# Layer 3's experts moved into the slots of layer 3's attention, with gelu built from tanh

## The chip, the cores and the metric

The kernel runs on one core of a Trainium2 chip. A core has a tensor engine for matrix products (PE, with its weight loads shown as PEld), a vector engine (DVE), a scalar engine for activation functions (ACT), a third elementwise engine (GpSimd, shown as POOL), and a queue that issues DMA transfers (SyncE, SP). The engines run side by side and wait for each other through semaphores. The metric is the device time of the whole program in microseconds (us); lower is better.

## What is computed

The input `x` has 2048 tokens of 256 numbers, and the context has 1601 rows of 256. Four layers follow each other. Each adds a cross attention and then a feed-forward part to `x`, both on a layer norm of `x`. The change concerns the last layer. Its attention has 16 heads of 16 numbers, and its mask leaves the last 400 context rows. Its feed-forward part has 8 experts; expert `e` handles the tokens 256e to 256e+255, so no routing is computed.

```python
def _L3_xattn_ref(query, key, value, mask, Wq, bq, Wk, bk, Wv, bv, Wo, bo):
    ...
    scores = jnp.einsum('bhqd,bhkd->bhqk', Q, K) / jnp.sqrt(jnp.float32(DK))
    scores = jnp.where(mask == 0, -jnp.inf, scores)
    weights = jax.nn.softmax(scores, axis=-1)
    attn = jnp.einsum('bhqk,bhkd->bhqd', weights, V)
    attn = attn.transpose(0, 2, 1, 3).reshape(b, -1, D)
    return attn @ Wo.T + bo

def _L3_ffn_ref(x, w1, b1, w2, b2):
    ...
    tokens = x.reshape(E, T, D)
    h = jnp.einsum('etd,edf->etf', tokens, w1) + b1[:, None, :]
    h = jax.nn.gelu(h)
    y = jnp.einsum('etf,efd->etd', h, w2) + b2[:, None, :]
    return y.reshape(B, S, D)
...
x = x + _L3_xattn_ref(_layernorm(x, axis=-1), ctx_1024, ctx_1024, mask, ...)
x = x + _L3_ffn_ref(_layernorm(x, axis=-1), L3_ffn_w1, L3_ffn_b1, L3_ffn_w2, L3_ffn_b2)
```

`jax.nn.gelu` is here the form with tanh, 0.5h(1 + tanh(0.79788(h + 0.044715h^3))).

## The kernel before

`x` stays on the chip as 16 tiles of 128 tokens. Four tiles make a chunk of 512 tokens, so there are four chunks, and each chunk holds the tokens of two experts. `norm` (L125) makes a chunk's layer norm: statistics on DVE (L132, L133), the inverse root on POOL (L135, L136), the normalised rows on DVE (L142), then eight transposes on PE (L161) through the `pm` bank, which ACT copies to `xnT` (L165).

`attention3_tail` (L1415) is layer 3's attention. A unit is one chunk and one group of four heads, so there are 16 units. A unit has four slots, one for each block of 100 context rows, hence 64 slots `n`, with `u, kt = divmod(n, 4)`. In each slot PE computes `scores` (L1564, four heads side by side into two score tiles `psc`), ACT takes `exp` of each of the two (L1571), and PE multiplies the exps of the previous slot by the values (`values`, L1581). Besides, each slot computes two pairs of row maxima for the token tile six ahead: `maxima` (matmul L1546 into a `psc` tile, DVE reduction L1550). Once per unit come `project` for the unit two ahead (L1531, copied twice by ACT, L1535 and L1536), `shift` (L1557, L1558), and `normalize` of the unit just ended (L1595): ACT copies its sums to `ri` (L1597), four `reciprocal` calls on DVE follow (L1604), and POOL multiplies (L1606). After a chunk's last unit come four `out_project` calls (L1614), which add to `x` (L1618 on POOL, L1619 on DVE). Finished unit ends wait in the lists `tasks`, `pieces` and `later`.

PE's order is the order in which the program states its instructions (`manual_schedule`, L1518); the order on the other engines is made by a scheduler from dependencies and the program's order. `banks` (L1517) divides PSUM: three score tiles of two banks each, one bank `pm` shared by project, shift, normalize, out_project and the norm's transposes, and one for the sums of values. The next chunk's norm is stated at once, at the slots 4, 20 and 36.

`ffn3` (L1649) runs after it. For each expert it loads `w1`, `w2` (1 MB each) and `b2` into one of three buffers, and for every second expert makes a chunk's norm. Per expert it does 8 column blocks of `w1` (L1702), gelu of each by one ACT instruction with the bias `b1` (L1706), then for the two token tiles the product with `w2` (L1713), adds `x + b2` (POOL L1718, DVE L1719) and stores `y` (L1720).

The core of the slot loop before is

```python
scores(u, kt)
maxima(n + 6, 0)
if last is not None:
    values(*last)
last = (u, kt)
maxima(n + 6, 1)
```

Of the kernel before, what the change touches and what calls it, by code (L numbers as in the profile page):

```python
# [8 lines left out]
F32 = mybir.dt.float32  # L9
# [3 lines left out]
ALU = mybir.AluOpType  # L13
# [40 lines left out]
class Net:  # L54
# [70 lines left out]
    def norm(self, c, row_scale=None, rms=False, split=None):  # L125


        nc = self.nc
        st = self.small.tile([P, TPC, 6], F32, name="st")
        mv = self.small.tile([P, TPC, 2], F32, name="mv")  # L130
        for i in range(TPC):
            nc.vector.bn_stats(st[:, i, :], self.x[c * TPC + i])  # L132
            nc.vector.bn_aggr(mv[:, i, :], st[:, i, :])  # L133
        rstd = self.small.tile([P, TPC], F32, name="rstd")
# [5 lines left out]
        for i in range(TPC):  # L140
# [4 lines left out]
            xns.append(xn)  # L145
        if rms:
# [5 lines left out]
            for i in range(TPC):  # L152
                nc.vector.tensor_scalar(xns[i], xns[i], ri[:, i : i + 1], None, ALU.mult)
        if split is None:
# [14 lines left out]
        return xnT  # L169
# [1245 lines left out]
    def attention3_tail(self, mask):  # L1415
# [6 lines left out]
        with ExitStack() as s:  # L1422
            kv = s.enter_context(tc.tile_pool(name="kv3", bufs=1))
            qp = s.enter_context(tc.tile_pool(name="q3", bufs=3))
            pp = s.enter_context(tc.tile_pool(name="p3", bufs=6))
# [45 lines left out]
            with ExitStack() as s0:  # L1471
# [7 lines left out]
                wvT = kv.tile([P, 2, D], F32, name="wvT")  # L1479
# [37 lines left out]
            self.banks(s, s=3, m=1, a=1)  # L1517
# [92 lines left out]
            def out_project(c, i):  # L1610
# [8 lines left out]
                nc.vector.tensor_tensor(x, ps[:, :D], x, ALU.add)  # L1619

            def normed(c):
                xnT[c] = self.norm(c)


            tasks, later, pieces = [], [], []
            normed(0)
# [8 lines left out]
            for n in range(U * TK):  # L1635
                u, kt = divmod(n, TK)
                scores(u, kt)
                maxima(n + 6, 0)
                if last is not None:
                    values(*last)  # L1640
                last = (u, kt)
                maxima(n + 6, 1)
                if kt == 0 and u + 2 < U:
                    project(u + 2)
# [5 lines left out]
                elif later:  # L1650
                    f, args = later.pop(0)
                    f(*args)
                    if kt == 3 and later:
                        f, args = later.pop(0)
                        f(*args)
                if pieces:
                    reciprocal(*pieces.pop(0))
                if n % (G * TK) == TK and u // G + 1 < NCH:
                    normed(u // G + 1)
            values(*last)  # L1660
            for f, args in tasks:
                f(*args)
            for args in pieces:
                reciprocal(*args)
            for f, args in later:
                f(*args)

# [56 lines left out]
def network(ctx: ExitStack, tc: tile.TileContext, a, out):  # L1724
# [7 lines left out]
    with tc.If(n_odd == 0) as masked:  # L1732
# [4 lines left out]
        net.attention3_tail(masks[1])  # L1737
        net.ffn3()
# [42 lines left out]
```

## Time and profile before

| | us |
|---|---|
| median of three runs | 2224.9 (2219.83 to 2228.75) |
| the profiled execution | 2223.65 |
| its span, first to last instruction | 2221.9 |
| layer 3's first scores | at 1778.3 |
| layer 3's last values end | at 2088.9 |

The mean granted clock of PE over the span is 0.936 of full speed. A group line of the profile names the source line, the engine, the operation and the tiles, then the busy time and the mean duration of one, then the idle time ahead of it and what ended it. The groups of layer 3 that matter most, over the part of the trace from 1500 us on:

```profile
L1571 ACT ACTIVATE p<-psc 100x1024 f32<-100x1024 f32 x128 | 125.5, 1023 | 110.1 <-PE psc L1564 104.5 <-PE psc L1546 5.5
L1550 DVE TENSOR_REDUCE ms<-psc 128x2 bf16<-128x800 f32 x128 | 124.1, 987 | 67.2 <-PE psc L1546 63.0 <-PE psc L1564 3.5
L1702 PE MATMUL psc<-xnT,w 128*128 128x256 f32 x256 | 57.5, 381 | 1.4 <-ACT h L1706 1.0 <-ACT xnT L165 0.2
L1713 PE MATMUL pa<-w,h 128*128 128x256 f32 x256 | 56.6, 379 | 0.0
```

One f32 matmul appears as two records. Records overlap on PE, so their mean duration is longer than their share of the time.

### The profile page before, as it was taken

How to read it: one execution, taken by the hardware profiler on the slowest of the kernel's cores; microseconds unless marked ns; L12 is line 12 of the kernel's file. 1: busy time of each engine (PE TensorE's matmuls, PEld its weight loads, DVE VectorE, ACT ScalarE, POOL GpSimd, SP SyncE). 2: the span in 40 equal slices, each digit the busy share in tenths (PEclk: the TensorE clock that was granted, in tenths of full speed). 3: DMA queues.
4: the chain of work that ended last, by engine and by line, in shares of the span. 5: the costliest groups of instructions: out<-in, count | busy, mean ns of one | idle time of the engine just before them, and what ended most of it. 6: DMA issues, size and time to landing. Idle time of an engine off the chain costs nothing.

```text
span 2221.9 us, 22832 instructions
## 1 busy us (share of the span) xinstructions
PE 1968.0 (89%) x8841; PEld 967.7 (44%) x8841; DVE 1209.1 (54%) x2252; ACT 717.5 (32%) x968; POOL 632.3 (28%) x405
## 2 busy tenths in 40 slices
PE   7789999999998677789897889999968788989899
PEld 3233333333334422234443674555557422333487
DVE  4565646555552599975645563222076557566500
ACT  4544434344443100000112442111143255455422
POOL 1168878777785000000000021000024401000100
PEclk9799999999998699999997899999978889799999
DMA  8820000000000000000201000000000000000351
GB/s 278 265 83 1 1 1 1 1 1 1 1 1 0 1 0 1 1 0 0 67 0 40 0 1 21 0 1 1 0 0 1 6 1 1 1 1 1 114 188 61
DMA packets 39698, 63.51 MB, mean 29 GB/s; under 512 B 5133, under 2 KB 32158, under 8 KB 39582
## 3 DMA queue, kind: packets, MB, share of 16 engines
q1 hardware_dynamic: 37776, 60.33, 8.4%
q10 hardware_dynamic: 1806, 1.64, 0.2%
q8 instruction: 71, 1.16, 0.2%
q14 instruction: 45, 0.37, 0.1%
HBM read 59.87 MB, written 2.10 MB: 28 GB/s over the span
## 4 chain that ended last, share of the span: by engine, by line
PE 66%; DVE 22%; ACT 4%; issue 3%; DMA 3%; POOL 2%; SPq 0%; DVEq 0%; ACTq 0%; POOLq 0%
PE pa L454 7%; PE psc L442 5%; PE psc L627 5%; PE psc L766 4%; PE pa L786 4%; DVE ge L576 4%; DVE mp L367 4%; PE psc L1564 3%; PE psc L1702 3%; DVE ge L578 2%; PE pa L1713 2%; DVE ri L404 2%; PE pa L1581 2%; DVE ri L1604 2%; PE pm L1614 2%
## 5 line engine op out<-in xcount | busy, mean ns | idle before, releaser
L463 POOL TENSOR_TENSOR sp<-sp,p 128x1024 f32<-128x1024 f32 (+1 forms) x176 | 418.9, 2380 | 59.6 <-ACT p L447 49.0
L367 DVE TENSOR_REDUCE mp<-pm 128x1 f32<-128x512 f32 x384 | 242.6, 679 | 161.4 <-PE pm L362 160.7
L447 ACT ACTIVATE p<-psc 128x1024 f32<-128x1024 f32 (+1 forms) x208 | 212.9, 1024 | 261.1 <-PE psc L442 167.0
L442 PE MATMUL psc<-qT,kT 64*128 64x512 f32 (+1 forms) x832 | 219.9, 591 | 0.0
L454 PE MATMUL pa<-p,v 128*64 128x512 f32 (+1 forms) x832 | 204.2, 613 | 0.0
L593 PE MATMUL psc<-ge,pick 128*8 128x512 bf16 x512 | 142.3, 378 | 37.9 <-DVE ge L576 18.6
L1571 ACT ACTIVATE p<-psc 100x1024 f32<-100x1024 f32 x128 | 125.5, 1023 | 110.1 <-PE psc L1564 104.5
L1550 DVE TENSOR_REDUCE ms<-psc 128x2 bf16<-128x800 f32 x128 | 124.1, 987 | 67.2 <-PE psc L1546 63.0
L362 PE MATMUL pm<-kb,qb 64*128 64x512 bf16 x384 | 100.2, 389 | 26.4 <-DVE mp L367 24.9
L1564 PE MATMUL psc<-q,kT 32*100 32x512 f32 x512 | 97.8, 689 | 14.8 <-DVE ms L1550 10.3
L627 PE MATMUL psc<-w_e,xe 128*128 128x512 f32 x256 | 110.4, 593 | 0.0
L454 PEld LDWEIGHTS pa<-p,v 128*64 128x64 f32 (+1 forms) x832 | 51.1, 137 | 131.6 <-issue 128.6
L135 POOL TENSOR_SCALAR rstd<-mv 128x4 f32<-128x4 f32 x32 | 10.5, 329 | 333.6 <-DVE mv L133 333.6
L829 POOL MEMSET v<- 128x4 f32 x1 | 0.1, 106 | 366.4 <-DVE n_odd L280 366.4
L766 PE MATMUL psc<-q,kT 128*128 128x512 f32 (+1 forms) x208 | 102.2, 610 | 0.0
L576 DVE TENSOR_SCALAR ge<-bc,g 128x128 bf16<-128x128 f32 (+15 forms) x128 | 99.8, 780 | 1.8 <-ACT bc L570 1.8
L142 DVE TENSOR_SCALAR xn<-x,mv,rstd 128x256 f32<-128x256 f32 x128 | 54.3, 482 | 75.0 <-PE pm L161 72.1
L442 PEld LDWEIGHTS psc<-qT,kT 64*128 64x128 f32 (+1 forms) x832 | 85.5, 185 | 19.5 <-issue 6.3
L786 PE MATMUL pa<-v,p 128*128 128x257 f32 (+1 forms) x416 | 93.9, 381 | 0.0
L593 PEld LDWEIGHTS <-pick 128*8 128x8 bf16 x512 | 39.4, 85 | 117.3 <-issue 91.3
L578 DVE TENSOR_SCALAR ge<-bc,g 128x1920 bf16<-128x1920 f32 (+14 forms) x120 | 89.4, 746 | 0.6 <-ACT bc L570 0.6
L440 PE MATMUL psc<-sh,negz 64*128 64x512 bf16 (+1 forms) x416 | 87.1, 383 | 2.6 <-ACT sh L389 2.5
(343 smaller groups left out, 3250.5 us busy)
## 6 DMA issues: line engine op xcount, KB each, us to landing
w<-in_L_ffn_w_dram SPq DMA_DIRECT2D x16, 1024.0 KB, 6.2
head<-in_mask_BxSxS_ik_dram SPq DMA_DIRECT2D x16, 600.5 KB, 4.7
head<-in_mask_1x1xSxS_ik_dram SPq DMA_DIRECT2D x16, 600.5 KB, 4.8
tail<-in_mask_BxSxS_ik_dram SPq DMA_DIRECT2D x16, 200.0 KB, 4.5
tail<-in_mask_1x1xSxS_ik_dram SPq DMA_DIRECT2D x16, 200.0 KB, 3.7
x<-in_x_dram SPq DMA_DIRECT2D x16, 128.0 KB, 3.7
w_e<-in_L_ffn_experts_dram SPq DMA_DIRECT2D x2, 1024.0 KB, 7.2
out_dram<-y SPq DMA_DIRECT2D x16, 128.0 KB, 2.7
```

Of the source, the lines that this page charges most:

```text
L367: nc.vector.tensor_reduce(mp[:, i, j, n : n + 1], pair[j][:, :wd], AX.X, ALU.max)
L442: nc.tensor.matmul(sc[:r, j, :], lhsT=kT[h, hp, kt * P : kt * P + r], rhs=q[h, :], start=False, stop=True,)
L447: nc.scalar.activation(p[:r], sc[:r], AF.Exp, scale=DH**-0.5)
L454: nc.tensor.matmul(acc[h, :], lhsT=v[:r, kt, hp * P + h.start : hp * P + h.stop], rhs=p[:r, j, :], start=kt == 0, stop=kt == NKT - 1,)
L463: nc.gpsimd.tensor_tensor(sums[:r], sums[:r], p[:r], ALU.add)
L576: nc.vector.tensor_scalar(ge[:, :hi], bc[:, :hi], own, None, ALU.is_lt)
L578: nc.vector.tensor_scalar(ge[:, hi:], bc[:, hi:], own, None, ALU.is_le)
L593: nc.tensor.matmul(rk[j // 2][0:E, j % 2, :], lhsT=pick[:, e, :], rhs=ge[:, j * CH : (j + 1) * CH], start=first, stop=last,)
L627: nc.tensor.matmul(sc[:, j, :], lhsT=xnT[t // TPC][:, kc, (t % TPC) * P : (t % TPC + 1) * P], rhs=ew[kc][:, half * 4 + 2 * j : half * 4 + ...
L766: nc.tensor.matmul(sc[:r, j, :], lhsT=kT[:, kc, ks], rhs=q[:, kc, :], start=kc == 0, stop=False)
L786: nc.tensor.matmul(acc[:, : D + 1], lhsT=p[:r, kt, i * P : (i + 1) * P], rhs=v[:r, kt, :], start=kt == 0, stop=kt == NKT - 1,)
L1564: nc.tensor.matmul(sc[j // 2][:TR, j % 2, :], lhsT=kT[h, g, kt * TR : (kt + 1) * TR], rhs=q[u][h, :], start=True, stop=True,)
```

## The change

`attention3_tail` becomes `layer3_tail`, and in this branch of the program `ffn3` is no longer called: the experts run inside the attention loop. When the last `out_project` of chunk `c` is stated, `feed_forward(c)` puts 38 steps into the list `fbits`: one `begin`, five `norm_step`, and for each of two experts eight `up` and eight `down`. Each slot takes two steps from it, by `feed(1)` between the two maxima and `feed(1)` at its end. What is left runs after the loop.

`up` writes one block's product into half of a PSUM tile of one bank; ACT adds the bias, and after each second block POOL makes z = h(0.044715h^2 + 1) in three instructions. `gelu` takes tanh on ACT and makes (tanh + 1)h on DVE. The missing factor 0.5 is applied in `end`, where DVE scales the sum. `down` adds one block's product for both token tiles in a second bank. To make room, the score tiles go from three to two, the p3 buffers from six to five, `wvT` borrows an `attn3` tile, and expert weights have two buffers instead of three; the first two experts are loaded ahead of the loop.

In a slot, `values` moves ahead of the first maxima, `reciprocal` to the top, and `out_project` is no longer confined to slots without another task. The layer norm becomes a generator of six steps, `norm_steps`; `norm` drains it. In the loop the next chunk's norm takes one step per slot from the slots 0, 16 and 32 on.

```diff
+    def norm_steps(self, c, out, row_scale=None, rms=False, split=None):
...
         for i in range(TPC):
             nc.vector.bn_stats(st[:, i, :], self.x[c * TPC + i])
             nc.vector.bn_aggr(mv[:, i, :], st[:, i, :])
+            if i % 2:
+                yield
...
             xns.append(xn)
+            if i == 1:
+                yield
...
+        yield
         if split is None:
             xnT = self.xnp.tile([P, 2, CH], F32, name="xnT")
...
+            if kc == 0:
+                yield
+        out.append(xnT)
...
-            pp = s.enter_context(tc.tile_pool(name="p3", bufs=6))
+            pp = s.enter_context(tc.tile_pool(name="p3", bufs=5))
...
-            self.banks(s, s=3, m=1, a=1)
+            self.banks(s, s=2, m=1, a=1)
+            psf = s.enter_context(tc.tile_pool(name="ps_f", bufs=1, space=bass.MemoryType.PSUM))
+            wp = s.enter_context(tc.tile_pool(name="f3w", bufs=2))
+            hp = s.enter_context(tc.tile_pool(name="f3h", bufs=2))
...
+            for e in range(2):
+                load_expert(e)
...
+                if i == TPC - 1:
+                    fbits.extend(feed_forward(c))
...
+                def up(e, f, k):
+                    w1 = experts[e][0]
+                    if k == 0:
+                        if f == 0:
+                            state["h"] = hp.tile([P, NF, 256], F32, name="h3")
+                        state["ps"] = psf.tile([P, 2, 256], F32, name="psu", tag="u")
+                    ps = state["ps"][:, k, :]
+                    for kc in range(2):
+                        nc.tensor.matmul(
+                            ps, lhsT=w1[:, kc, (f + k) * P : (f + k + 1) * P],
+                            rhs=out[0][:, kc, (e % 2) * 256 : (e % 2 + 1) * 256],
+                            start=kc == 0, stop=kc == 1,
+                        )
+                    at = e * NF + f + k
+                    h = state["h"][:, f : f + 2, :]
+                    nc.scalar.activation(h[:, k, :], ps, AF.Identity, bias=b1[:, at : at + 1])
+                    if k == 1:
+                        z = hp.tile([P, 2, 256], F32, name="z3")
+                        nc.gpsimd.tensor_tensor(z, h, h, ALU.mult)
+                        nc.gpsimd.tensor_scalar(z, z, 0.044715, 1.0, ALU.mult, ALU.add)
+                        nc.gpsimd.tensor_tensor(z, z, h, ALU.mult)
+                        gelus.append((h, z))
...
+                def down(e, f, k):
...
+                    for i in range(2):
+                        nc.tensor.matmul(
+                            acc[:, i, :], lhsT=state["h"][:, f + k, i * P : (i + 1) * P], rhs=w2[:, f + k, :],
+                            start=f + k == 0 and i == 0, stop=f + k == NF - 1 and i == 1,
+                        )
...
+                def end(e):
...
+                        nc.gpsimd.tensor_tensor(y, self.x[t], b2, ALU.add)
+                        nc.vector.scalar_tensor_tensor(y, state["acc"][:, i, :], 0.5, y, ALU.mult, ALU.add)
+                        nc.sync.dma_start(self.out[0, t * P : (t + 1) * P, :], y)
+                    if e + 2 < E:
+                        load_expert(e + 2)
...
+                for e in (2 * c, 2 * c + 1):
+                    for f in range(0, NF + 4, 2):
+                        for k in range(2):
+                            if f < NF:
+                                yield up, (e, f, k)
+                        for k in range(2):
+                            if f >= 4:
+                                yield down, (e, f - 4, k)
+
+            def gelu():
+
+                if gelus:
+                    h, z = gelus.pop(0)
+                    nc.scalar.activation(z, z, AF.Tanh, scale=0.7978845608028654)
+                    nc.vector.scalar_tensor_tensor(h, z, 1.0, h, ALU.add, ALU.mult)
...
             for n in range(U * TK):
                 u, kt = divmod(n, TK)
+                if pieces:
+                    reciprocal(*pieces.pop(0))
                 scores(u, kt)
-                maxima(n + 6, 0)
                 if last is not None:
                     values(*last)
                 last = (u, kt)
+                maxima(n + 6, 0)
+                feed(1)
                 maxima(n + 6, 1)
+                gelu()
...
-                elif later:
+                if later:
                     f, args = later.pop(0)
                     f(*args)
...
-                if pieces:
-                    reciprocal(*pieces.pop(0))
-                if n % (G * TK) == TK and u // G + 1 < NCH:
-                    normed(u // G + 1)
+                feed(1)
+                if n % (G * TK) == 0 and u // G + 1 < NCH:
+                    norming = self.norm_steps(u // G + 1, xn)
+                step(norming, 1)
...
+            while pieces:
+                reciprocal(*pieces.pop(0))
+                feed(2)
+                gelu()
...
+            while fbits:
+                ready = len(gelus)
+                feed(2)
+                for _ in range(ready):
+                    gelu()
...
-        net.attention3_tail(masks[1])
-        net.ffn3()
+        net.layer3_tail(masks[1])
```

## The prediction

> **What bounds the kernel now.** I first read the page's busy shares and its 40 slices. The tensor engine (PE) carries the program, and its granted clock sags just where the change works (slices 33 to 37).
>
> ```profile
> PE 1968.0 (89%) x8841; PEld 967.7 (44%) x8841; DVE 1209.1 (54%) x2252; ACT 717.5 (32%) x968; POOL 632.3 (28%) x405
> PEclk9799999999998699999997899999978889799999
> ```
>
> Then I found the starts of layer 3's 64 attention slots in the timeline and asked for busy time over three stretches: slots 0 to 24, slots 25 to 63 with the last values, and the rest.
>
> ```profile
> 1778.30:1901.30 123.00, 109.85 (x590) 33.64 (x590) 76.92 (x92) 65.91 (x78) 12.28 (x13) 0.86 0.00 1
> 1901.30:2088.90 187.60, 171.53 (x937) 58.27 (x936) 114.03 (x149) 97.26 (x115) 16.46 (x16) 0.90 0.00 1
> 2088.90:2221.90 133.00, 124.28 (x580) 104.55 (x579) 19.31 (x45) 36.94 (x75) 14.10 (x19) 1.00 0.47 151
> ```
>
> Columns: length, then busy PE, weight load, DVE, ACT, POOL; clock; DMA. The stage is 443.6 us. In the loop PE is busy for 281.4 of 310.6 us, but at a clock of 0.86 to 0.90; the expert stretch runs at 1.00 with 9 us idle. So the loop's slack is some 29 us of idle PE and what the low clock adds. Last, the timeline of one unit shows which waits make the slots:
>
> ```profile
> 1852.74 2.22 PE L1564 MATMUL psc<-q,kT 32*100 32x512 f32 x8
> ...
> 1858.97 1.12 PE L1564 MATMUL psc<-q,kT 32*100 32x512 f32 x8
> ...
> 1860.24 1.94 ACT L1571 ACTIVATE p<-psc 100x1024 f32<-100x1024 f32 x2
> 1860.31 1.00 DVE L1550 TENSOR_REDUCE ms<-psc 128x2 bf16<-128x800 f32 x1 [2.14 <-PE psc L1546]
> ...
> 1863.43 3.39 DVE L1604 RECIPROCAL ri<-ri 128x128 f32<-128x128 f32 x4 [0.74 <-ACT ri L1597]
> ...
> 1866.74 1.83 DVE L1550 TENSOR_REDUCE ms<-psc 128x2 bf16<-128x800 f32 x2
> ...
> 1867.73 1.10 PE L1564 MATMUL psc<-q,kT 32*100 32x512 f32 x4 [0.76 <-DVE ms L1550]
> ```
>
> Scores take 1.12 us at full clock and 2.22 at half. Two exps take 1.94, one maxima reduction 1.00. The four reciprocals, issued one per slot, run as one block of 3.39 us; the reductions queue behind it, and half of a later score group waits for them.
>
> **What the Trainium skill says.** "TensorE: Matmul & The Clock Gate", Part 1: the clock has two values, half and full, and idle windows of about 3.4 us bring half. The trace agrees on the values (5 us windows show 0.50 and 1.00; 2.22 against 1.12 us). "ScalarE: Activation LUTs", Table sets: tanh sits with exp, gelu in another set, a load takes 1283 ns. The trace shows that load at L1706 (1283 ns), with 1.36 us ahead of it; tanh beside exp isn't in this trace. "GPSIMD Engine Reference", 4.1 Engine selection: two-input elementwise work is about twice as slow there as on VectorE, one-input work about equal. Here L1606 (two inputs, 128x512) took 1266 ns and the one-input cast at L672 616 ns. "PSUM — Partial Sum Buffer", section PSUM: the matmul accumulator: eight banks of 2 KB a partition. Before, 3x2+1+1 used all; the two banks for experts come from the third score buffer.
>
> **The change, part by part.** Full-clock PE durations: scores 1.12, values 1.06, one maxima pair 0.34, project 1.98, shift 0.40, normalize 1.12, out_project 1.75 (eight records of 0.216), one expert step 0.866 (L1702: 32 records in 6.93).
>
> *Third score buffer removed, values moved ahead of maxima.* A slot allocates four tiles, so each of two buffers now runs scores, exp, maxima, reduction, scores. From a slot's start: scores end 1.12, first exp 1.18 to 2.15, second to 3.12, values end 2.18. Maxima 0 starts at 2.22: its wait is hidden by values. Maxima 1 waits for the second exp, 3.17 to 3.50, and everything later in PE's fixed order queues behind it. Its reduction ends at 4.6, and only then can the second half of the next scores start. An empty slot therefore takes 4.6 us where before it took 3.2 (starts 1793.96, 1797.16).
>
> *Slots without experts.* Chunk 0's last out_project falls in slot 24, so slots 0 to 24 have no filler. A unit costs: kt 0 with project 5.5 plus 0.26 for q/qb ahead of the exps; kt 1 with normalize 4.65; kt 2 6.15; kt 3 4.6; sum 21.1. The 6.15 contains 1.5 for the reciprocal block: its call moves to the slot's top, but one call per slot was in the code before too and the trace still has four in a row, so I expect the block to stay (3.4 us from about 0.7 after normalize). 6.25 units give 132; slot 0's table load and start 4; the two norms' transposes, still behind project and normalize in the one pm bank, 6.5; four out_projects less the slack they fill 6.5. Sum 149, against 123: **+26**.
>
> *Slots with experts.* Slots 25 to 63 take two steps each; with one at slot 24, 79 in all, of which 18 are norm steps and 61 up or down. PE sum: scores 43.7, values 41.3, 33x2 maxima 22.4, 7 projects 13.9, 9 shifts 3.6, 10 normalizes 11.2, 8 out_projects 14.0, transposes 5.3, steps 52.8 = 208. The first step covers the second exp and the second step most of the last reduction (a shift slot has 5.0 us of PE work), so the ring mostly disappears. Left are about 1.8 us a unit where kt 2 and kt 3 end at 4.6 to 5.0 and DVE has a gelu product or reciprocal in front of a reduction (10 units, 18), out_project waiting for the pm bank (8x0.9, 7), and four norms (9). Sum 243, against 188: **+55**. DVE carries about 4.1 of 6.2 us a slot, ACT 3.4, POOL 2.2; none is the bound.
>
> *Tail.* After 81 steps (two more follow the loop), 33 of chunk 2 and 38 of chunk 3 remain, 64 of them up or down, with one normalize and four out_projects: 19.5 us until the last out_project, 12 steps among them. Then gelu is exposed. Identity 0.47, POOL 1.27+0.65+1.27=3.2 plus handovers, tanh 0.6, DVE 0.68: some 5.5 us from a pair of ups to its downs. PE's order has only two pairs of ups in between for the first pair, 3.5 us; POOL's 3.3 us a pair exceeds the others' spacing. Written out, downs start at 7.2, 10.7, 13.8 and 17.1 and the expert ends at 18.8 us, against 13.85 of PE work. Sum: 19.5 + 5.3 (rest of one expert) + 18.8 + 2.8 (chunk 3's transposes) + 2x18.8 + 4 (last product and output) = 88, against 133: **-45**. Gelu's table load is in the old 133 and gone.
>
> *At nothing:* expert weights, two loaded ahead of the loop and two buffers after: each 1 MB load lands in 6.2 us, the expert before it lasts over 13.85. On SP they queue behind the two y stores; exposed, one would cost up to 12. The p3 buffers fall to five; four are live, so none is waited for; a wait would cost an exp, 1 us. wvT's borrowed tile is read before the loop. The other layers' norms are drained whole, as before.
>
> **Sum.** +26 +55 -45 = +36 on the profiled execution's 2223.65 (span 2221.9 and 1.75 around it) = 2260; the runs' median, 2224.9, is 1.25 above that execution, inside their spread, so 2260 stands.
>
> **Unknown costs.** Clock in the bare slots: all full 132+8 and less for early half-started scores, down to 132; half the time at half clock, with PE work of 5.7 and a slot of 6.2, up to 160. Expert slots: 215 with nearly no waits, 262 with DVE late in each slot. POOL's tensor_scalar: 0.62 (L672) to 1.27 (L1606), taken 0.65; tanh 0.59 to 0.69, taken 0.6; the SBUF product 0.47 (half its size, L1192) to 0.70, taken 0.68. Tail from 80 (waits filled) to 102 (1.27 on POOL, some half clock). All low: 427, -17; all high: 524, +80.
>
> **Rivals.**
> 1. *DVE keeps slot order, so PE never waits for a buffer* (0.19). One mechanism, on DVE in the loop: reciprocals stand singly at a slot's top, while scores and values run, and every maxima reduction starts as its matmul ends. Bare units lose the 1.5 us of the block (6.25x1.5=9) and a first half that starts early takes 3 more: 137. Fed slots lose the 18 of late reductions, and 12 of the 16 for pm, whose releasing adds no longer queue: 213. The tail's products come at once: 81. Sum 431, -13, so 2211. For it: DVE is busy for only 191 of 310 us in the loop. Against: the block of four in the trace. It decides once the waits of the whole stage fall below 55 us (PE work 98 bare + 208 + 66 + 5 for the shared ends = 377, and 443.6-11-377); I count 103.
> 2. *Even* (0.09): fed slots at 228, bare ones at 133 and tail 83 give 444.
> 3. *Cold and late* (0.17): bare slots oscillate at half clock (160), DVE's added products delay every second reduction (258), POOL at 3.9 a pair holds the tail at 98: 516, +72, 2296. For it: windows with under 4 us of PE work in 5 were followed by 0.50 at 1850 and 2035. Against: the same at 1950 was not.
> 4. *As worked out* (0.55): 2240 to 2280. That the experts aren't interleaved at all is excluded by PE's fixed order.
>
> **Numbers.** Faster by over 0.5% (11 us, what a measurement here can tell from none) 0.19, within 0.09, slower 0.72. The range cuts 1 in 10 at either end: 2207 to 2300; the likeliest case alone is 2240 to 2280.
>
> **What would show it.** Right: bare slots 4.6 to 6 us apart, with PE's maxima waiting for the exp and scores for DVE; fed slots near 6.2 at a clock over 0.95; last values near 2170; downs waiting for DVE h in the tail. Wrong: slots 0 to 24 in about 125 us, or reciprocals standing singly, or a tail at 1.00 clock with no waits. It would also fall if another engine's order makes fed slots longer than 7 us.

## The result, and the profile after

The changed kernel takes 2343.91 us (median of four runs, 2341.55 to 2346.92). The kernel before takes 2223.51 beside it (four runs, 2219.83 to 2228.75). The ratio is 1.054, with an interval of 1.0514 to 1.0567. So the direction was forecast, but the loss is 120 us instead of 36, and it lies outside the range.

The profiled execution of after took 2346.92 us, with a span of 2345.2. This is its line of busy times and its granted clock in 40 slices:

```profile
PE 2014.9 (86%) x8831; PEld 977.8 (42%) x8841; DVE 1231.8 (53%) x2284; ACT 732.7 (31%) x999; POOL 726.3 (31%) x501
PEclk9799999999995999999979899998887679999888
```

PE has lost no work and gained none to speak of (8841 records before, 8831 after). Yet it is busy for 47 us more, since much of that work runs at a lower clock: in layer 3's slices the lowest digit is now 6, where it was 7, and the last slices read 8 instead of 9. POOL has 94 us more, which is gelu's polynomial (32 pairs of about 2.95 us). Cutting layer 3 at the same three points as before (first scores, scores of slot 25, end of the last values) gives this view of busy time by stretch. Its columns are stretch, length, then busy PE, weight load, DVE, ACT and POOL, clock, DMA share and rate:

```profile
1777.00:1944.50 167.50, 135.23 (x603) 41.02 (x603) 76.40 (x100) 67.21 (x80) 9.90 (x10) 0.77 0.00 1
1944.50:2224.50 280.00, 236.02 (x1194) 103.16 (x1194) 133.00 (x181) 121.39 (x165) 72.15 (x76) 0.93 0.11 34
2224.50:2345.20 120.70, 83.61 (x308) 60.69 (x306) 23.35 (x45) 27.69 (x54) 56.22 (x60) 0.89 0.17 53
```

| stretch, us | before | forecast | after | after against forecast |
|---|---|---|---|---|
| slots 0 to 24 | 123.0 | 149 | 167.5 | +18.5 |
| slots 25 to 63, last values | 187.6 | 243 | 280.0 | +37.0 |
| the rest ("the tail") | 133.0 | 88 | 120.7 | +32.7 |
| layer 3 | 443.6 | 480 | 568.2 | +88.2 |

The column "before" comes from the profiled execution of before. No stretch was forecast well; all three err to the same side. Each has its own mechanism, and each shows in the timeline. First, a stretch of slots without expert steps (start, duration, instruction; in brackets the idle time ahead of it and what ended it):

```profile
1842.46 3.39 DVE L1637 RECIPROCAL ri<-ri 128x128 f32<-128x128 f32 x4 [0.66 <-ACT ri L1630]
...
1845.77 1.83 DVE L1583 TENSOR_REDUCE ms<-psc 128x2 bf16<-128x800 f32 x2
...
1846.76 2.92 PE L1597 MATMUL psc<-q,kT 32*100 32x512 f32 x8 [1.15 <-DVE ms L1583]
...
1849.61 1.94 PE L1614 MATMUL pa<-p,v 100*32 100x512 f32 x8
...
1853.11 2.93 PE L1597 MATMUL psc<-q,kT 32*100 32x512 f32 x8 [1.11 <-DVE ms L1583]
```

These lines show the four reciprocals still in one block, the reduction behind them, and the scores behind the reduction, since both score tiles are taken. After that wait, scores take 2.92 us with the waits inside them and values 1.94; at full clock they took 1.12 and 1.06. The next scores find the clock still low.

Second, a slot with expert steps:

```profile
1983.95 1.93 PE L1597 MATMUL psc<-q,kT 32*100 32x512 f32 x8
...
1986.17 1.27 POOL L1691 TENSOR_TENSOR z<-z,h 128x512 f32<-128x512 f32 x1
...
1987.47 0.63 ACT L1734 ACTIVATE z<-z 128x512 f32<-128x512 f32 x1 [4.46 <-POOL z L1691]
1988.01 1.92 ACT L1604 ACTIVATE p<-psc 100x1024 f32<-100x1024 f32 x2
...
1989.06 0.34 PE L1579 MATMUL psc<-kb,qb 32*128 32x400 bf16 x2 [2.19 <-ACT p L1604]
```

The scores were complete at 1985.9, but their exps start only at 1988.0. ACT had stood idle for 4.46 us at the tanh of L1734, which waited for POOL's z. The exps were queued behind it, and then PE's maxima behind the exps. The view of waits between 1941 and 2224 (total, times, longest) counts ACT's waits for z, and PE's waits of its maxima for the exps:

```profile
ACT z L1734 <- POOL z L1691: 47.7, 16, 5.0
PE psc L1579 <- ACT p L1604: 17.5, 27, 2.4
```

Third, the tail, between two blocks of `w1`, and the waits of PE from 2223 to the end:

```profile
2264.86 1.13 PE L1679 MATMUL psu<-xnT,w 128*128 128x256 f32 x4 [0.56 <-ACT h L1686]
...
2266.32 0.63 ACT L1734 ACTIVATE z<-z 128x512 f32<-128x512 f32 x1 [1.50 <-POOL z L1691]
2266.85 0.46 ACT L1686 ACTIVATE h<-psu,b 128x256 f32<-128x256 f32 x1
...
2267.36 2.07 PE L1679 MATMUL psu<-xnT,w 128*128 128x256 f32 x4 [1.37 <-ACT h L1686]
```

```profile
PE psu L1679 <- ACT h L1686: 22.4, 24, 2.5
PE psy L1700 <- DVE h L1735: 5.0, 3, 1.7
```

PE mostly waits ahead of an up, for ACT's bias copy of the block just made, and hardly ahead of a down. Both kinds of up wait: the second half of a pair, since its tile is still being read, and the first half of the next pair, since there is only one such tile. Once the bias copy also stands behind a tanh, PE waits 1.37 us and then runs at half clock (2.07 for the same four records that took 1.13).

### The profile page after: what moved, and what is told of

It is laid out like the page before. It is cut to its first block, busy times and chain, and to the rows that moved or that the text cites. A ratio compares the mean times of both kernels' runs of the same rounds, so it can differ in the third digit from the quotient of the medians.

```text
span 2345.2 us, 22958 instructions
## 1 busy us (share of the span) xinstructions
PE 2014.9 (86%) x8831; PEld 977.8 (42%) x8841; DVE 1231.8 (53%) x2284; ACT 732.7 (31%) x999; POOL 726.3 (31%) x501
## 5 line engine op out<-in xcount | busy, mean ns | idle before, releaser
L1583 DVE TENSOR_REDUCE ms<-psc 128x2 bf16<-128x800 f32 x128 | 122.8, 990 | 142.2 <-PE psc L1579 142.2
L1597 PE MATMUL psc<-q,kT 32*100 32x512 f32 x512 | 100.4, 719 | 18.9 <-DVE ms L1583 18.9
L1679 PE MATMUL psu<-xnT,w 128*128 128x256 f32 x256 | 80.1, 439 | 23.1 <-ACT h L1686 22.7
```

What stands on the lines that cost most here:

```text
L1583: nc.vector.tensor_reduce(ms[u % 2][:, i, 64 * k + DH : 64 * k + 64 : 32], ps[:, :, :NTAIL], AX.X, ALU.max)
L1679: nc.tensor.matmul(ps, lhsT=w1[:, kc, (f + k) * P : (f + k + 1) * P], rhs=out[0][:, kc, (e % 2) * 256 : (e % 2 + 1) * 256], start=kc == 0, ...
```

## The experiments

All but E9 and E12 are single executions with a profile. They are read by stretch. Slots 0 to 24 took 167.5 us in after and in three variants (E1, E2 and E6) that leave them untouched, and 167.6 in E10. They repeat less well where the clock changes from unit to unit: E5 and E7 run the same instructions in the same order on every engine there and took 150.0 and 146.5 us. The totals carry more: layer 3's first scores came between 1767.1 us (E8) and 1779.1 us (E9), although no variant touches what lies before them, so single totals are not compared to better than some 12 us. The kernel before ran at 2216.84 to 2221.22 beside them (medians, or one run). The times of before, after, E9 and E12 are medians, their stretches those of one profiled execution. All stretches in one place:

| us | slots 0-24 | 25-63 | tail | time |
|---|---|---|---|---|
| before | 123.0 | 187.6 | 133.0 | 2223.51 |
| after | 167.5 | 280.0 | 120.7 | 2343.91 |
| E1 halves in two banks | 167.5 | 279.9 | 119.0 | 2342.79 |
| E2 ACT in stated order | 167.5 | 246.3 | 114.5 | 2303.49 |
| E3 before, two score tiles | 158.2 | 227.5 | 139.2 | 2297.48 |
| E4 filler on PE | 160.7 | 279.9 | 120.4 | 2331.8 |
| E5 DVE in stated order | 150.0 | 287.0 | 150.6 | 2361.83 |
| E6 a tile for each up | 167.5 | 281.8 | 110.2 | 2336.56 |
| E7 E2 + E5 + E6 | 146.5 | 261.1 | 138.7 | 2324.82 |
| E8 before, DVE in stated order | 118.4 | 165.8 | 135.4 | 2188.44 |
| E9 E8 + norm in six steps | 107.8 | 161.8 | 135.2 | 2183.17 |
| E10 E2 + E6 + second y buffer | 167.6 | 246.1 | 104.7 | 2295.88 |
| E11 E5 in the loop + filler | 150.0 | 288.1 | 134.5 | 2349.63 |
| E12 all repairs | 113.3 | 254.8 | 103.1 | 2245.54 |

**E1, the halves of an up pair in two banks.** After the loop, the score tiles are free. A pair of ups takes one of them, so its halves lie in different banks of one tile.

```diff
-state["ps"] = psf.tile([P, 2, 256], F32, name="psu", tag="u")
+state["ps"] = self.psc()[:, :, :256] if tail else psf.tile([P, 2, 256], F32, name="psu", tag="u")
```

> The changed kernel, but after the slot loop each expert block goes into a bank of its own (the score tiles, free by then) instead of half of one shared bank. Theory 'shared bank': in the stretch after the loop (122 us) every up waits for ACT's bias copy of the up before it, because both halves lie in one bank; PE's waits there on ACT h fall from 22 us to under 6 and the total falls by 20 to 30 us, to about 2320. Rival 'gelu latency' (POOL's three instructions and tanh set the tail): downs take over the wait, PE waits on DVE h grow to over 15 us, and the total falls by under 8 us.

The tail went from 120.7 to 119.0 us. In E1's timeline the same wait stands ahead of the same instruction:

```profile
2259.12 0.47 ACT L1686 ACTIVATE h<-psc,b 128x256 f32<-128x256 f32 x1 [10.58 <-PE psc L1679]
...
2259.65 1.99 PE L1679 MATMUL psc<-xnT,w 128*128 128x256 f32 x8 [0.56 <-ACT h L1686]
```

So it isn't the bank, and neither theory held: in the tail of E1 PE waits 26.4 us for the bias copies, in 16 waits, against 22.4 in 24 in after. The waits of first halves are gone, since the next pair has another tile, and those of second halves got longer. In after the two halves share a bank, and "PSUM — Partial Sum Buffer", section PSUM bank collisions raise a hardware error, says that a TensorE write and a ScalarE read of one bank must be kept apart. That would make a wait necessary in after, which no run here tests, but it doesn't explain this one: here the banks differ, and the 0.56 us is still there. What remains in common is that both halves are one tile in the program. E6 tests that.

**E2, the exps ahead of the tanh.** ACT's order is the stated one, and `gelu` moves to before the first expert step.

```diff
-s.enter_context(tc.manual_schedule(engines={PE}))
+s.enter_context(tc.manual_schedule(engines={PE, Activation}))
...
 maxima(n + 6, 0)
+gelu()
 feed(1)
 maxima(n + 6, 1)
-gelu()
```

> The changed kernel with ACT held to the stated order as PE is, and tanh stated ahead of the slot's first expert step, so behind the slot's two exps and a slot after its POOL work began. Theory 'tanh blocks ACT': in slots 25 to 63 exps stand behind a tanh that waits for POOL (ACT waits 48 us on POOL z there); that wait falls under 10 us, those slots shrink from 279 us to about 250, total 2315. Rival 'PE clock and pm bank' (fed slots are long because PE is at half clock at times and pm has one bank): the slots stay within 8 us of 279. Slots 0 to 24 hold no tanh and stay at 165 to 170 under both.

Slots 25 to 63 fell from 280.0 to 246.3 us, and slots 0 to 24, which have no tanh, stayed at 167.5. In E2's timeline the tanh now comes after the exps and finds its z ready:

```profile
1967.99 1.94 ACT L1604 ACTIVATE p<-psc 100x1024 f32<-100x1024 f32 x2 [0.36 <-PE psc L1597]
...
1969.81 0.63 ACT L1734 ACTIVATE z<-z 128x512 f32<-128x512 f32 x1
```

PE's wait of its maxima for the exps, 17.5 us in 27 waits in after, is 5.0 us in 25 waits in E2:

```profile
PE psc L1579 <- ACT p L1604: 5.0, 25, 0.6
```

ACT's wait for z, 47.7 us in after, no longer appears in the fed slots (those that take expert steps) at all, and the clock of the stretch rises from 0.93 to 0.97. The edit changes the place of the tanh and the rule for ACT's order together, and the rule covers the bias copies too, so their shares aren't told apart. That ACT's order as a whole costs 34 us here is shown.

**E3, the kernel before with two score tiles**, and with `values` ahead of both maxima as in after.

```diff
-self.banks(s, s=3, m=1, a=1)
+self.banks(s, s=2, m=1, a=1)
...
-maxima(n + 6, 0)
 if last is not None:
     values(*last)
 last = (u, kt)
+maxima(n + 6, 0)
 maxima(n + 6, 1)
```

> The kernel before with nothing but two score tiles instead of three and values ahead of the first maxima; no experts in the loop. Theory 'two buffers make bare slots long': slots 0 to 24 take 160 to 170 us as in the changed kernel (123 before), with a clock under 0.80, and the total rises by 90 to 110 us, since all 64 slots are bare, to about 2320. Rival 'the new layout of norms, reciprocals and out_projects makes them long': slots 0 to 24 stay under 140 and the total under 2270.

Slots 0 to 24 went from 123.0 to 158.2 us, the other slots from 187.6 to 227.5, and the kernel takes 2297 us. The total rose by 76 us, less than the 90 to 110 expected. So two tiles, with the moved values, cost 35 us in the slots without experts, with no expert, tanh or norm step of the change in the program, and they take the clock there from 0.86 to 0.76:

```profile
1770.80:1929.00 158.20, 131.26 (x590) 37.95 (x590) 74.45 (x91) 65.67 (x78) 12.26 (x13) 0.76 0.00 1
```

**E4, filler on PE.** The first 24 slots of after get two f32 matmuls each between the maxima; nothing reads their product.

```diff
+def filler():
+    ps = psf.tile([P, 2, 256], F32, name="psu", tag="u")
+    for kc in range(2):
+        nc.tensor.matmul(ps[:, 0, :], lhsT=experts[0][0][:, kc, :P], rhs=wqT[:, kc, 0:256], start=kc == 0, stop=kc == 1)
...
 maxima(n + 6, 0)
+if n < 24:
+    filler()
```

> The changed kernel with a dummy product of 0.87 us, read by nobody, between the two maxima of each of slots 0 to 23 (21 us of added PE work at full clock). Theory 'half clock': the idle gaps there bring PE to half clock (0.77 over slots 0 to 24), and filling them brings it above 0.90, so slots 0 to 24 get shorter than 167 us by 8 to 25 although work was added. Rival 'ring alone' (buffers set the slots whatever the clock): they stay at 165 to 170. If PE work were the bound they would grow by about 20 to 27.

A filler is as large as one expert step, 0.866 us at full clock by the forecast's figure, so 24 of them add 20.8 us of PE work. The slots became 6.8 us shorter:

```profile
1769.10:1929.80 160.70, 142.16 (x699) 53.36 (x699) 78.19 (x100) 67.56 (x80) 9.91 (x10) 0.93 0.00 1
```

PE is busy for 142.2 us instead of 135.2, with 96 records more, because all of it runs at 0.93 instead of 0.77. The gain is somewhat under what the half-clock theory asked for, but its sign is that theory's: a part of the 167.5 us is the clock, not waits. DVE, ACT and POOL run the same instructions in the same order there as in after, so it isn't another order. The gain lies where the clock became full. The last whole unit before the experts (slots 16 to 19), in after and in E4:

```profile
1877.61:1901.84 24.23, 20.46 (x91) 5.45 (x91) 11.41 (x14) 10.08 (x12) 1.26 (x1) 0.71 0.00 0
1867.31:1888.69 21.38, 20.05 (x108) 7.12 (x106) 11.71 (x13) 10.15 (x12) 1.26 (x1) 1.00 0.00 1
```

**E5, DVE in stated order** in the whole of layer 3, so that each reciprocal stands at the top of a slot of its own.

```diff
-s.enter_context(tc.manual_schedule(engines={PE}))
+s.enter_context(tc.manual_schedule(engines={PE, DVE}))
```

> The changed kernel with DVE held to the stated order, as PE is: one reciprocal at the top of a slot instead of up to four in a row. Theory of the prediction (the block costs a bare unit about 1.5 us): slots 0 to 24 fall from 167.5 to about 158, slots 25 to 63 by 5 to 15 from 280. Rival 'the ring and the clock make the bare slots, the block only shifts': slots 0 to 24 stay within 4 us of 167.5.

Slots 0 to 24 fell to 150.0 us, and the clock there rose from 0.77 to 0.85:

```profile
1772.60:1922.50 149.90, 125.07 (x603) 38.61 (x603) 76.79 (x104) 67.19 (x80) 14.37 (x17) 0.85 0.00 1
```

The block of reciprocals, with the low clock that goes with it, is thus worth 17.5 us, or 2.8 for each of the 6.25 units; E11 parts the two. The fed slots as a whole gained nothing (287.0), and the tail lost 30 us. PE's waits from 2200 on name the place:

```profile
PE pm L172 <- DVE xn L150: 20.9, 2, 12.2
```

A norm is now stuck on DVE; E7 shows behind what.

**E6, a PSUM tile for each up after the loop.** As E1, but each half takes a score tile of its own.

```diff
-state["ps"] = psf.tile([P, 2, 256], F32, name="psu", tag="u")
-ps = state["ps"][:, k, :]
+state["ps"] = None if tail else psf.tile([P, 2, 256], F32, name="psu", tag="u")
+ps = self.psc()[:, 0, :256] if state["ps"] is None else state["ps"][:, k, :]
```

> The changed kernel, but after the loop every expert block gets a score tile of its own, so two blocks no longer share a tile. The run before it gave the halves separate banks inside one tile, and PE still waited at each second half. Theory 'shared tile': the wait goes with the tile, PE's waits on ACT h after the loop fall under 8 us, and the stretch (121 us) falls by 10 to 20. Rival 'tanh ahead of the bias copy in ACT's queue': the wait stays at over 15 us, since the copy itself is late behind a tanh that waits for POOL, and the stretch falls by under 5 us.

The tail fell from 120.7 to 110.2 us. The wait of the ups for ACT, 22.4 us in after, is gone from the list, and the downs wait instead. This is the first line of PE's waits from 2226 on:

```profile
PE psy L1700 <- DVE h L1735: 17.1, 7, 3.4
```

E1 also has two tiles to take turns with, so beside it this shows that the wait follows the tile. The downs' wait for gelu, which was forecast, had been hidden behind the other one.

**E7, the edits of E2, E5 and E6 together.**

```diff
-s.enter_context(tc.manual_schedule(engines={PE}))
+s.enter_context(tc.manual_schedule(engines={PE, Activation, DVE}))
...
```

> The changed kernel with ACT and DVE both in stated order, tanh a slot later, and a score tile of its own for each expert block after the loop. If the three causes are separate, their gains add: slots 0 to 24 about 158 to 167, slots 25 to 63 about 240, after the loop about 95 to 100, total about 2275. If the tail is set by gelu's latency (5.5 us from ups to downs) alone, the last stretch stays above 108.

They don't add. Slots 0 to 24 are at 146.5 us, but the fed slots only at 261.1 and the tail at 138.7. The timeline of the tail shows why DVE's order hurts there:

```profile
2262.46 0.72 POOL L1712 TENSOR_TENSOR y<-x,b 128x256 f32<-128x256 f32 x1 [9.59 <-DMA out_dram<-y]
...
2263.22 0.42 DVE L1713 SCALAR_TENSOR_TENSOR y<-psy,y 128x256 f32<-128x256 f32 x1 [6.44 <-POOL y L1712]
2263.56 0.42 DVE L138 BATCH_NORM_STATS2 st<-x 128x6 f32<-128x256 f32 x1
```

There is one `y` buffer. The second token tile's sum waits on POOL until the first has been stored; DVE's part of it waits 6.44 us for POOL, and the next norm's statistics, which need neither, come right behind it in the stated order. The same wait stands in the fed slots. By the trace of E7, DVE stood at the `y` sum for 6.3 to 6.7 us in slots 36, 44 and 54, and these took 14.4, 12.4 and 17.8 us, where E2 has 7.8, 5.9 and 8.5. That is 22 us, more than the 15 by which E7 is behind E2. E5 lost 20 us in the same three slots against after. So DVE's order wasn't bad for the other fed slots; no run gave it a second `y` buffer there.

**E8, the kernel before with DVE in stated order**, and nothing else.

```diff
-s.enter_context(tc.manual_schedule(engines={PE}))
+s.enter_context(tc.manual_schedule(engines={PE, DVE}))
```

> The kernel before with nothing but DVE held to the stated order in the attention loop, so its reciprocals stand one to a slot. The theory that the block of four holds up score tiles there as well (DVE's reciprocals carry a good part of the chain of waits): the loop falls from 310.6 us by 8 to 25, total 2200 to 2215. Rival: the norm, stated at one point, now blocks the maxima behind it, and the total is not below 2220.

2188.44 us, 31 less than the run beside it. Layer 3 itself became 24 us shorter (419.6 against 443.6); the rest lies before it, where nothing was changed. Slots 25 to 63 went from 187.6 to 165.8 us and slots 0 to 24 from 123.0 to 118.4. The block of reciprocals was thus a loss in the kernel before already, and it can be taken away without moving an expert.

**E9, E8 with the six-step norm** of the change, one step a slot from the slots 0, 16 and 32 on.

```diff
 if kt == 0 and u + 2 < U:
+    if xn:
+        xnT[u // G + 1] = xn.pop()
     project(u + 2)
...
-if n % (G * TK) == TK and u // G + 1 < NCH:
-    normed(u // G + 1)
+if n % (G * TK) == 0 and u // G + 1 < NCH:
+    norming = self.norm_steps(u // G + 1, xn)
+step(norming, 1)
```

> The kernel before with DVE in stated order in the attention loop and the next chunk's norm in six steps, one to a slot, as in the change; no experts in the loop, three score tiles. DVE's order alone gave 2188. Theory 'a norm stated at once holds up DVE and PE' (the slots of the norms took 11.7 to 13.1 us there): the three norm slots fall to about 6, the total to 2170 to 2180. Rival 'the pm bank makes those slots long however the norm is stated': within 5 us of 2188.

Median 2183.17 us (four runs, 2179.67 to 2185.6), against 2220.67 for the kernel before on the same chip (seven runs, 2207.97 to 2223.79). The ratio is 0.9842, with an interval of 0.9798 to 0.9886. This beats both kernels. The view by stretch, and a piece of the timeline at the same point of a unit as the one of after above:

```profile
1779.10:1886.90 107.80, 96.15 (x586) 31.14 (x586) 77.75 (x104) 65.29 (x78) 13.64 (x16) 0.95 0.00 1
1886.90:2048.70 161.80, 150.15 (x937) 51.85 (x936) 116.30 (x166) 96.40 (x115) 21.85 (x23) 0.99 0.00 1
```

```profile
1839.61 0.95 DVE L1617 RECIPROCAL ri<-ri 128x128 f32<-128x128 f32 x1 [0.73 <-ACT ri L1610]
...
1840.48 2.02 DVE L1563 TENSOR_REDUCE ms<-psc 128x2 bf16<-128x800 f32 x2
...
1842.02 1.12 PE L1577 MATMUL psc<-q,kT 32*100 32x512 f32 x8 [0.24 <-ACT p L1584]
...
1843.01 0.94 DVE L1617 RECIPROCAL ri<-ri 128x128 f32<-128x128 f32 x1
```

One reciprocal a slot, the reduction behind one instead of four, and scores at 1.12 us. The totals of E8 and E9 are only 5 us apart, which looks like the rival, but E8 began layer 3 12 us earlier. Layer 3 itself takes 404.8 us against 419.6, and the slots show that this is the norm: slots 4, 20 and 36, where E8 states a whole norm, took 11.7, 12.5 and 13.1 us, and in E9 6.5, 7.5 and 7.5.

**E10, E2 and E6 together, and a second `y` buffer in the tail.**

```diff
-y = hp.tile([P, D], F32, name="y", bufs=1)
+y = op.tile([P, CH], F32, name="o3")[:, :D] if tail and i else hp.tile([P, D], F32, name="y", bufs=1)
```

> The changed kernel with ACT in stated order and tanh a slot later, a score tile of its own for each expert block after the loop, and there a second buffer for y; DVE is left to the scheduler. Theory 'the last stretch is long by shared tiles, tanh ahead of bias copies and one y buffer' (121 us, of which I had worked out 88): slots 0 to 24 stay at 167.5, slots 25 to 63 at 246, the last stretch comes to 90 to 100, total about 2280. Rival 'gelu's latency and the half clock it brings': the last stretch stays above 105.

The tail is at 104.7 us. E2 alone took 6.2 us off it and E6 alone 10.5; together that would be 104.0, so the second `y` buffer adds nothing that shows. What is left, in E10's timeline and in PE's waits from 2184 on:

```profile
2255.81 3.68 PE L1700 MATMUL psy<-w,h 128*128 128x256 f32 x8 [2.51 <-DVE h L1735]
```

```profile
PE psy L1700 <- DVE h L1735: 17.0, 9, 2.5
```

Gelu's chain is exposed, as forecast. Of the nine waits, three were followed by eight slow records (3.68 us after a wait of 2.51, 3.75 after 1.58, 2.75 after 2.34), the other six, of up to 2.50 us, by eight at full clock (1.99 us). So a wait can bring a low clock with it, but mostly didn't.

**E11, E5's order in the slot loop only, and E4's filler.**

```diff
+held = s.enter_context(ExitStack())
+held.enter_context(tc.manual_schedule(engines={PE, DVE}))
...
+held.close()
+held.enter_context(tc.manual_schedule(engines={PE}))
 values(*last)
```

> The changed kernel with DVE in stated order in the slot loop only (so not after it), and the dummy product of 0.87 us in slots 0 to 23. Theory 'ring plus reciprocal block plus half clock': with the block gone (150 us for slots 0 to 24 when alone) and the clock above 0.93 by the filler, slots 0 to 24 take 138 to 146 although 21 us of work is added. Rival 'no clock effect once the block is gone': 150 or more. Slots 25 to 63 come near 285 as under DVE's order alone, the last stretch near 121.

In sum the filler brings nothing and costs nothing:

```profile
1775.30:1925.30 150.00, 136.30 (x699) 52.20 (x699) 79.03 (x104) 67.44 (x80) 14.41 (x17) 0.97 0.00 1
```

E5 had 149.9 us at a clock of 0.85 in the same slots. That looks like the rival, "no clock effect once the block is gone", but single units say otherwise. Two units of E5 (slots 8 to 11 and 16 to 19) and one of E11 (slots 8 to 11):

```profile
1820.26:1842.90 22.64, 20.11 (x90) 5.15 (x91) 11.74 (x14) 10.20 (x12) 1.26 (x1) 0.73 0.00 1
1863.48:1881.63 18.15, 15.89 (x90) 4.39 (x90) 14.22 (x24) 10.07 (x12) 4.04 (x5) 1.00 0.00 0
1823.16:1843.64 20.48, 19.97 (x109) 7.13 (x107) 12.09 (x13) 10.24 (x12) 1.27 (x1) 1.00 0.00 0
```

With the same PE records, a unit takes 22.64 us at a clock of 0.73 and 18.15 at 1.00. So the clock is worth 4.5 us a unit without the block too. The four fillers of a unit cost about 2.3 us where the clock is full already (20.48 against 18.15). Over the 25 slots the two cancel, by chance. The units also give the block's own price at full clock: 21.38 us with it (E4 above) against 20.52 without it in slots 16 to 19 of E11, both with fillers, so 0.9 us a unit.

Releasing DVE after the loop brought the tail from 150.6 to 134.5 us, but not to the 120.7 of after. The largest wait left lies at the end of the loop, and it is E7's again: DVE stands at a `y` sum, and PE waits for the norm behind it.

```profile
2217.84 0.42 DVE L1714 SCALAR_TENSOR_TENSOR y<-psy,y 128x256 f32<-128x256 f32 x1 [8.20 <-POOL y L1713]
...
2224.21 1.45 PE L172 MATMUL pm<-ident,xn 128*128 128x128 f32 x4 [10.82 <-DVE xn L150]
```

**E12, every repair at once.** Three score tiles and stated order on PE, ACT and DVE for slots 0 to 24; from slot 25 on two tiles, and PE and ACT in stated order with the moved `gelu`; after the loop E6's tiles and E10's buffer.

```diff
+held.enter_context(tc.manual_schedule(engines={PE, Activation, DVE}))
 for n in range(U * TK):
+    if n == 25:
+        held.close()
+        self.ps_s = held.enter_context(tc.tile_pool(name="ps_s2", bufs=2, ...))
+        psf = held.enter_context(tc.tile_pool(name="ps_f", bufs=1, ...))
+        held.enter_context(tc.manual_schedule(engines={PE, Activation}))
...
```

> The changed kernel with every cause found so far taken away at once, experts still in the slots: three score tiles and DVE in stated order for slots 0 to 24 (two tiles and the experts' banks from slot 25 on), ACT in stated order throughout with tanh a slot later, a score tile of its own for each expert block after the loop and a second buffer for y there. Theory 'found causes explain the loss, but interleaving itself gains nothing' : slots 0 to 24 take 108 to 120, slots 25 to 63 246, the last stretch 100 to 105, total 2235 to 2255, that is, still 15 to 30 us above the kernel before. Rival 'interleaving pays once the orders are mended': below 2210.

Median 2245.54 us (four runs, 2244.17 to 2247.6) against 2216.84 (seven runs): the ratio is 1.0133, with an interval of 1.0099 to 1.0168. By stretch:

```profile
1772.40:1885.70 113.30, 102.45 (x596) 32.38 (x596) 78.17 (x107) 64.06 (x77) 15.66 (x18) 0.94 0.00 1
1885.70:2140.40 254.70, 232.38 (x1202) 102.22 (x1203) 134.94 (x194) 122.84 (x167) 73.32 (x77) 0.95 0.12 37
2140.40:2243.50 103.10, 74.14 (x307) 58.21 (x306) 25.74 (x45) 27.51 (x54) 57.49 (x59) 0.95 0.20 61
```

Against the kernel before beside it, the loss falls from 120 to 29 us, and the kernel is still slower than before. The third tile is worth some 33 us in slots 0 to 24 (146.5 in E7, with the same orders on PE, ACT and DVE, 113.3 here), close to the 35.2 of E3. In slots 25 to 63 PE is busy for 232.4 of 254.7 us, against 171.5 of 187.6 before. So the experts' work has lengthened the slots by about its own length, 67 us for 61 us of PE, and the tail gave back only 30: PE has 50 us less work there, but is idle for 29 us instead of 9, waiting for gelu above all. The fed slots still have two score tiles here, and 7 of their 254.7 us come with the exchange of tiles (slots 25 to 27 took 25.6 us, against 18.9 in E2).

## Why the prediction was right or wrong

**The sign: right, and for the reason that was ranked first.** A ring of two score tiles and a loop without room for the experts were to cost more than the tail would give back. E3 shows the ring alone. E12 shows how little room there is, with PE busy for 232 of 255 us, though its fed slots keep the ring of two. Before, PE was idle for only 16 us in slots 25 to 63, and the expert stretch already ran at a clock of 1.00 with 9 us idle, so the interleaving had little to fill.

**Slots 0 to 24, +26 forecast, +44.5 measured.** The waits were right: scores wait for DVE's reduction (1.15 and 1.11 us in the timeline), and the block of four stayed. The step that failed is the clock: the sum of 149 takes every PE duration at full clock. A unit was put at 21.1 us, 1.5 of it for the block; in slots 8 to 19 after's units took 24.2 to 24.9 us at a clock of 0.71. At full clock ring and block were rather put too high: a unit with two tiles and no block takes 18.15 us (E5), where 19.6 were forecast, and the block adds 0.9 (E4 against E11). But both lower the clock: two tiles from 0.86 to 0.76 (E3), and without the block it rises from 0.77 to 0.85 (E5). The bound of 160, taken from half the time at half clock, was itself too low. The cited rule, that idle windows of about 3.4 us bring half clock, doesn't cover this case: in slots 8 to 19 of after PE was never idle for more than 1.21 us.

**Slots 25 to 63, +55 forecast, +92.4 measured.** The step that failed reads "DVE carries about 4.1 of 6.2 us a slot, ACT 3.4, POOL 2.2; none is the bound." The shares are about right (ACT is busy for 121.4 us in 39 slots, which is 3.1 each), and they were the wrong thing to add up. ACT executes what is at the head of its queue. "PSUM — Partial Sum Buffer", section Engine vs sequencer instructions, calls ScalarE's queue a strict FIFO, and the trace agrees: exps whose scores were complete at 1985.9 waited until 1988.0 behind a tanh whose z was on POOL. The change added that wait, and I had not named what is queued behind it. E2 gives ACT's order as 34 of the 37 us by which the sum was short; with it repaired the stretch takes 246.3 us, near the 243 worked out from PE's steps. One of its counts was off: the stretch holds 64 up or down steps (128 PE records of each kind), not 61, which adds 2.6 us. How its 35 us of waits split was not shown, so luck may have part in the agreement.

**The tail, -45 forecast, -12.3 measured.** The durations were right. A pair costs POOL 1.06 + 0.62 + 1.27 = 2.95 us by the groups of after against 3.2 forecast, tanh takes 0.63 against 0.6 and the product 0.69 against 0.68. No table load stands at L1734, so gelu's load did go. The failed step is the written-out expert of 18.8 us, which let PE make two pairs of ups ahead. PE could not: each up waited for ACT's copy of the up before it, since the two halves of a pair are one tile and there was only one such tile. That is 10.5 us by E6, and 6.2 more are ACT's order by E2. Some 17 us remain over 88 in E10 (104.7). The downs' waits for gelu (17.0 us there) are mostly not the excess, since the 88 already held some 22 us beside 66 us of PE work. In E10 PE is busy for 76.5 us, at a clock of 0.92, and idle for 28.2: about 10 us more work time, which the low clock explains in part, and 6 more of waiting. No run isolated these. "y at nothing" held for the time of after as it stands, since a second buffer changed nothing that shows, but by the traces of E5, E7 and E11 the single buffer is what makes DVE's stated order costly; no run in that order had a second one.

**The rivals.** "DVE keeps slot order" (2211) didn't happen by itself, and E5 forced it: 150.0 for the 137 it claimed, 287.0 for 213, 150.6 for 81. So in this program it would not have come out faster either, though the single `y` buffer has a part in that. It looked at the queue that had a visible block in the trace of before, and the new block was on ACT. "Cold and late" (2296) had the half clock in bare slots right, and even its 160 was below the 167.5 measured. For the fed slots it named DVE's added products, and E2 shows that the larger delay was on ACT.

**What would show it.** Of the signs named ahead: bare slots (those without expert steps) were 6.7 us apart on average (167.5 / 25), above the 4.6 to 6; the fed slots at 7.2 us (280.0 / 39) crossed the 7 us named as "another engine's order", and it was another engine's order; the last values came at 2224.5 and not near 2170; the downs' wait for DVE appeared in full only once the ups were freed (E6).

## What to carry to other kernels

When work is moved between the instructions of a tuned loop, list for every engine, not for PE alone, what then stands at the head of its queue waiting, and who is behind it: ACT's order around a 0.63 us tanh cost 34 us here, on an engine busy for less than half of the time. Stating an engine's order has the same danger: a sum that waits for a single buffer then holds up everything behind it (E7). Before filling a loop, count what PE leaves idle in it; here PE was busy for nine tenths of the stretch, moved work lengthened it by about its own length, and the buffer given up for it cost some 33 us on top. And look first at the order of the engine whose block already shows in the trace: holding DVE to its stated order, with the norm in steps, made the kernel before 1.6% faster (1.1 to 2.0%) with no expert moved.

## What the runs showed of the hardware that was not expected

- More PE work made a stretch shorter. Two matmuls more in each of 24 slots raised the clock of the stretch from 0.77 to 0.93, and its length fell from 167.5 to 160.7 us, with the same order on every other engine (E4). Such filler has its price: a unit of E5 that ran at 1.00 without it took 18.15 us, one of E11 with it 20.48.
- PE was granted a clock of 0.71 in slots 8 to 19 of after, although none of its gaps there was longer than 1.21 us.
- A wait on PE is sometimes paid twice: in the tail of E10 eight records took 3.68 us after a wait of 2.51, and 1.99 after another of 2.50.
- PE's matmul into one half of a PSUM tile waited 0.56 us for ACT's read of the other half even with the halves in different banks (E1), and not with two tiles (E6). The wait is one that the program's tiles bring, not the banks.
